# Attention on one Trainium2 core: weighted sums two key tiles behind the scores, and the transposed steps moved to the end of the turn

## The chip, the cores and the metric

The kernel runs on one core of one Trainium2 chip. The metric is the device time of one execution in microseconds (us). Before the change it is 7679.73 us, the median of three runs (7679.41 to 7688.48). The profile below is of one further execution, with a span of 7673.1 us.

The engines are named as the profile names them: PE is TensorE (matmuls), PEld its weight loads, DVE is VectorE, ACT is ScalarE, POOL is GpSimd, and SP the engine that issues DMAs.

## The reference, cut to what matters

The reference is two layers over four images of 128 channels by 64x64 pixels, that is 4096 tokens of 128 values for each image: a convolutional attention, then a multi-head attention with a feed-forward, then a recurrent layer over all tokens. The change touches only the multi-head attention:

```python
B, S, H, D = ...              # 4 images, S = 4096 tokens, 16 heads of D = 8
q      = transpose(_qz_ring(heads + rx_theta))           # queries, keys and values are the same q
scores = einsum('bhsd,bhtd->bhst', q, q) / sqrt(D)
attn   = softmax(scores, axis=-1)
ctx    = einsum('bhst,bhtd->bhsd', attn, q)
```

Queries and keys are the same vectors, so the matrix of scores of a head is symmetric. The kernel uses that: the exponentials of one off-diagonal pair of blocks are computed once, and serve the other one transposed. No maximum is subtracted ahead of the exponential.

## The kernel before, in words

**Stages.** For each of the four images, `first_stage` does the convolutional attention (with the feed-forward of the image before it in between), and `second_stage` does the multi-head attention by calling `attention` (L523). After the last image come `third_stage` and the recurrence. Inside the stages the order of TensorE, ScalarE and VectorE instructions (in the attention GpSimd's too) is exactly the order in which the Python code emits them (`manual_schedule`)[...].

**Blocks and turns.** The attention runs over 8 pairs of heads, and in each pair over 4 query blocks `b` of 1024 queries. A block meets its own 8 key tiles of 128 keys ("own" tiles), and the key tiles of the one or two blocks in `behind[b]` ("off" tiles): blocks 0 and 1 meet 16 off and 8 own tiles, in the order off, off, own; blocks 2 and 3 meet 8 and 8, in the order off, own. That is 80 tiles in a pair. One pass through the inner loop (L790), for one key tile and two heads, is called a **turn** here. In this version the instructions of a turn are emitted in this order:

1. **S**, the scores (L800): four matmuls of 32 rows, in four row tiles of the array at once, into two PSUM tiles `ss` of 128x1024, one for each head. The pool `ps_pair` has three such tiles.
2. Two exponentials on ScalarE (L809), one for each head, into `es`. Off tiles also leave a sum (`accum_out`, shown as ACTIVATION_READ_ACCUMULATOR). The `es` tiles come round again after five turns.
3. **M**, transposed ("mirror") steps (L661), through `run_pending`: the sums that the transposed exponentials give to the other block. Four off tiles make a group, and a group has 16 steps of four matmuls each, in four column tiles of the array; in float32 each is recorded as two matmuls. `credit` says how many steps a turn may run: an own turn adds 2 and an off turn 3, at most 4 are held, and what isn't used is carried over. The last step of a group is followed by a copy or an addition on VectorE that takes the sums out of PSUM (`later <- misc`, L672 or L674). The groups alternate between two halves of one tile `misc`.
4. **W**, the weighted sums (L679) of the tile of the turn before, `weigh(before)`: four matmuls (eight records) with four column tiles, into `acc`, which accumulates over the block. `ps_acc` has one tile. After a block's last tile `finish` (L703) is called; it starts with a VectorE transpose of `acc` into `o` (L707), and GpSimd then sorts the parts.
5. **Flips**, `run_flips` (L639): VectorE's 32x32-wise transposes (L648) of this turn's exponentials, if the tile is an off tile. They are what M of a later turn reads. On a block's last tile no flips are emitted.

[...]`ps_pair` holds three tiles of two banks, `ps_acc` and `ps_misc` one bank each.

Of the kernel before, what the change touches and what calls it, by code (L numbers as in the profile page):

```python
# [26 lines left out]
def kernel(  # L27
# [31 lines left out]
    nc = tc.nc  # L59
# [50 lines left out]
    def get(kind, name):  # L110
        if callable(here[kind]):
            return here[kind](name)
        pool, shape = here[kind]
        return pool.tile(shape, F32, tag=kind, name=name)
# [7 lines left out]
    def half_tile(name):  # L122
        return get("half", name)
# [399 lines left out]
    def attention(n, q, xs, tail, upcoming):  # L523
# [10 lines left out]
        fixed, _ = here["fixed"]  # L534
# [88 lines left out]
        def run_pending(turn, count):  # L623


            taken = 0
            if pending and pending[0][0] <= turn:
                steps = pending[0][1]
                while steps and taken < count:
                    steps.pop(0)()  # L630
                    taken += 1
                if not steps:
                    pending.pop(0)
            return taken
# [4 lines left out]
        def run_flips(most):  # L639
            while most and flips:  # L640
                g, k, es = flips[0]
                if g >= 2 and groups[g - 2]["steps"]:
                    return
                group = groups[g]
                if k == 0:
                    group["e"] = [get("flipped", f"t{group['name']}_{h}") for h in range(2)]
                for h in range(2):
                    nc.vector.transpose(group["e"][h][:, k, :], es[h])  # L648
                if k == TG - 1:
                    pending.append((turn + 1, group["steps"], group["block"]))  # L650
                flips.pop(0)
                most -= 1
# [21 lines left out]
                    nc.vector.tensor_tensor(dst, dst, state["acc"], ALU.add)  # L674

        def weigh(it):
            for h in range(2):
                for x in range(2):
                    nc.tensor.matmul(  # L679
                        it["acc"][ts(2 * h + x, 32), :],  # L680
                        it["qa"][:, ds((2 * it["jt"] + h) * V, 32)],
                        it["e"][h][:, ts(x, IC)],
                        start=it["first"],
                        stop=it["last"],
                        skip_group_check=True,
                    )

        def mirrored_sums(pair, b, denom):

            total = denom[:, 0, ts(b, QT), :]  # L690
            for slot in range(1, len(met_by[b])):
                by_key = small.tile([P, QT, 2], F32, tag="by_key", name=f"by_key{n}_{pair}_{b}")
                nc.gpsimd.tensor_tensor(by_key, total, denom[:, slot, ts(b, QT), :], ALU.add)
                total = by_key
            by_token = small.tile([P, QT, 2], F32, tag="by_token", name=f"by_token{n}_{pair}_{b}")
            src = total.rearrange("p (x s) h -> p s x h", s=4)
            dst = by_token.rearrange("p (x a) h -> p a x h", a=4)
            for a in range(4):
                for s in range(4):
                    nc.gpsimd.tensor_copy(dst[ts(s, 32), a], src[ts(a, 32), s])  # L700
            return by_token

        def finish(pair, b, acc, later, denom):  # L703


            o = half_tile(f"o{n}_{pair}_{b}")
            nc.vector.transpose(o, acc)  # L707

            tag = "own" if b else "own_0"
            own = once.tile([P, QT, 2, V], F32, tag=tag, name=f"own{n}_{pair}_{b}")  # L710
            ov = o.rearrange("p (s a m) -> p s a m", s=4, a=4)
            for h in range(2):
                for x in range(2):
                    for s in range(4):
                        nc.gpsimd.tensor_copy(  # L715
                            own[ts(s, 32), ts(x, 4), h, :], ov[ts(2 * h + x, 32), s, :, 0:V]
                        )

            def mirrored():
                while any(g["steps"] and g["block"] <= (pair, met_by[b][-1]) for g in groups):  # L720
                    run_flips(TG)
                    run_pending(turn + 2, 16)
                sums = mirrored_sums(pair, b, denom)


                turned = get("turned", f"turned{n}_{pair}_{b}")
                nc.vector.transpose(turned, later[:, ts(b, 2 * P)])  # L727
                tv = turned.rearrange("p (y k a d) -> p k y a d", y=2, k=4, a=4)
                other = once.tile([P, QT * 2 * D], F32, tag="other", name=f"other{n}_{pair}_{b}")
                to = other.rearrange("p (y a h d) -> p h y a d", y=2, a=4, h=2)  # L730
                for x in range(2):
                    for h in range(2):
                        for k in range(4):
                            nc.gpsimd.tensor_copy(to[ts(k, 32), h], tv[ts(2 * h + x, 32), k])  # L734
                    at = other.rearrange("p (t h d) -> p t h d", h=2, d=D)
                    nc.gpsimd.tensor_tensor(own[:, :, :, 0:D], own[:, :, :, 0:D], at, ALU.add)
                nc.gpsimd.tensor_tensor(own[:, :, :, D], own[:, :, :, D], sums, ALU.add)

            def result():
                inv = small.tile([P, QT, 2], F32, tag="inv", name=f"inv{n}_{pair}_{b}")  # L740
                nc.vector.reciprocal(inv, own[:, :, :, D])
                nc.vector.tensor_tensor(
                    qb[:, ts(b, QT), ts(pair, 2 * D)].rearrange("p t (h d) -> p t h d", d=D),
                    own[:, :, :, 0:D],
                    inv.unsqueeze(3).broadcast_to([P, QT, 2, D]),
                    ALU.mult,
                )

            if b:
                ends.append((turn, mirrored))  # L750
                ends.append((turn + 6, result))
            else:
                first.extend([mirrored, result])

        def order(b):

            own = list(range(QT * b, QT * (b + 1)))
            rest = [jt for k in behind[b] for jt in range(QT * k, QT * (k + 1))]
            each = len(rest) // QT
            return [  # L760
                jt for k in range(QT) for jt in rest[each * k : each * (k + 1)] + own[k : k + 1]
            ]
# [5 lines left out]
                return [get("exps", f"e{name}_{h}") for h in range(2)]  # L768
            return [xs[:, ts(2 * k + h, QB)] for h in range(2)]

        before = None
        turn = 0

        credit = 0.0
# [1 line left out]
        ends, first = [], []  # L776
# [3 lines left out]
        for pair in range(NPAIR):  # L780
            keys, queries, qa, later, denom = ready
            for b in range(NQB):
                acc = get("ps_acc", f"acc{n}_{pair}_{b}")
                tiles = order(b)
                end_of_all = pair == NPAIR - 1 and b == NQB - 1

# [3 lines left out]
                for at, jt in enumerate(tiles):  # L790
# [27 lines left out]

                    if at == 1:
                        credit = 4.0  # L820
                    credit -= run_pending(turn, int(credit))
                    turn += 1
                    while ends and ends[0][0] < turn:
                        ends.pop(0)[1]()
                    if before is not None:
                        weigh(before)
                        if before["last"]:
                            finish(*before["block"])

                    if b == 0 and at == 10 and pair:  # L830
                        ends.append((turn, first.pop(0)))
# [23 lines left out]
                            groups.append(group)  # L855
                        flips.append((len(groups) - 1, jt % TG, es))

                    if jt != tiles[-1]:
                        run_flips(2)
                    for _ in range(3 if tail and turn == 2 else 1):  # L860
                        if tail and turn > 1 and next(tail, tail) is tail:
# [1 line left out]
                            rest()  # L863
                    if end_of_all and at in (QT, QT + 6) and upcoming:
                        upcoming.pop(0)()
                    before = {
                        "acc": acc,
                        "qa": qa,
                        "jt": jt,
                        "e": es,  # L870
                        "first": jt == tiles[0],
                        "last": jt == tiles[-1],
                        "block": (pair, b, acc, later, denom),
                    }
                assert not coming
                w = w_next
            if pair + 1 < NPAIR:
                ready = upcoming_pair
        weigh(before)
        finish(*before["block"])  # L880
        for f in upcoming:
            f()
        while flips or pending:
# [250 lines left out]
    def second_stage(im, tail, upcoming):  # L1134
# [33 lines left out]
        with stage(f"attn{n}", sides, others, **pools):  # L1168
            engines = {e.engine for e in (nc.tensor, nc.scalar, nc.vector, nc.gpsimd)}
            with tc.manual_schedule(engines=engines):  # L1170
                im["left"] = attention(n, im["q"], im["xs"], tail, upcoming)
# [30 lines left out]
    before = None  # L1202
    x_next = {"xs": load_x(0, ts(0, P))}
    for n in range(N):
# [12 lines left out]
        before = image  # L1217
# [22 lines left out]
    with stage("runs", t2=((P, 2 * IC), 4 * N), half=(HALF, 2 * NS + 1), ps_one=(ONE, 2 * NS)):  # L1240
# [34 lines left out]
        with tc.manual_schedule(engines={nc.tensor.engine, nc.scalar.engine}):  # L1275
# [3 lines left out]
            for t in range(-WARM, L):  # L1279
                for k in range(NS):  # L1280
                    acc = wx[k].rearrange("p (n i c) -> p n i c", n=NN, c=IC // L)
# [145 lines left out]
```

## Time and profile before

| stretch of the span, us | what | length, us | PE busy, us | ACT busy, us | DVE busy, us |
|---|---|---|---|---|---|
| 446 to 1761 | attention, image 0 | 1315 | 1299.30 | 1275.00 | 973.81 |
| 2330 to 3636 | attention, image 1 | 1306 | 1288.60 | 1262.92 | 966.19 |
| 4206 to 5509 | attention, image 2 | 1303 | 1288.00 | 1262.47 | 964.53 |
| 6076 to 7388 | attention, image 3 | 1312 | 1294.41 | 1266.07 | 970.05 |
| the rest | convolution, feed-forward, recurrence | 2437 | | | |

The four attention stretches are 5236 us of the 7673.1 us, and the change concerns only these. PE's busy time in the profile is modelled, since matmuls are pipelined; a PE that is shown busy for 99% of a stretch need not be at its peak. The better measure is how far apart the first score matmuls of two successive turns start: that is the length of a turn on TensorE. In the same way, the distance between the starts of two exponentials is what ScalarE takes for one. Wait lines read "engine, waiting line <- engine, line waited for: us in total, times, longest".

### The profile page before, as it was taken

The numbers are of one execution on the slowest core, as the hardware profiler recorded it, in microseconds if no ns is written. First come the engines' busy times: TensorE is split into PE (matmuls) and PEld (weight loads), VectorE is DVE, ScalarE is ACT, GpSimd is POOL, SyncE is SP. The second block draws the span as 40 slices with busy tenths as digits, with TensorE's granted clock in tenths as the row PEclk, the third lists the DMA queues.
The fourth block names the chain that finished last, engine by engine and source line by source line (L and its number), as shares of the span: only waits on it lengthen the run. The fifth ranks groups of instructions, "written<-read, shape, count | busy, mean of one in ns | idle before, by whom it ended". The sixth has DMA issues, their size and how long they took to land. (4 is left out here: it accounts for less than half of the span.)

```text
span 7673.1 us, 211342 instructions
## 1 busy us (share of the span) xinstructions
PE 7342.2 (96%) x87566; PEld 3334.3 (43%) x87566; DVE 5561.2 (72%) x7344; ACT 6146.6 (80%) x9493; POOL 2769.3 (36%) x9796
## 2 busy tenths in 40 slices
PE   8999999999999999999899999999999999999976
PEld 3334444444444444444444444444444444444445
DVE  5777777776787777777678777777677877777754
ACT  4479999995448999999444999999844699999964
POOL 1134444343223433343323343444322334444341
PEclk9999999999999999999999999999999999999987
DMA  0010000000111000000011000000001100000012
GB/s 26 25 42 23 25 19 20 19 9 24 33 44 36 25 20 19 23 21 16 18 33 46 32 20 19 22 23 17 17 25 34 52 20 23 23 25 19 11 53 102
DMA packets 81501, 211.92 MB, mean 28 GB/s; under 512 B 8768, under 2 KB 8800, under 8 KB 79760
## 3 DMA queue, kind: packets, MB, share of 16 engines
q1 hardware_dynamic: 77312, 186.68, 7.1%
q8 instruction: 689, 11.29, 0.6%
q10 hardware_dynamic: 2016, 10.49, 0.3%
q14 instruction: 284, 2.33, 0.1%
q0 software_dynamic: 1200, 1.14, 0.1%
HBM read 141.65 MB, written 56.62 MB: 26 GB/s over the span
## 5 line engine op out<-in xcount | busy, mean ns | idle before, releaser
L809 ACT ACTIVATE e<-s 128x1024 f32<-128x1024 f32 x3104 | 3068.5, 1027 | 117.1 <-PE s L800 104.8
L648 DVE STREAM_TRANSPOSE t<-e 128x1024 f32<-128x1024 f32 x1872 | 2201.4, 1218 | 653.4 <-ACT e L809 635.8
L809 ACT ACTIVATE xs<-s 128x1024 f32<-128x1024 f32 x2016 | 1993.0, 1025 | 49.4 <-PE s L800 46.3
L661 PE MATMUL misc<-t,mirror 128*32 128x128 f32 x49152 | 1817.9, 278 | 55.4 <-DVE later L672 27.6
L679 PE MATMUL acc<-e,q_aug 128*32 128x512 f32 x12416 | 1700.9, 595 | 0.0
L648 DVE STREAM_TRANSPOSE t<-xs 128x1024 f32<-128x1024 f32 x1200 | 1413.2, 1218 | 357.8 <-ACT xs L809 346.0
L661 PEld LDWEIGHTS misc<-t,mirror 128*32 128x32 f32 x49152 | 1225.5, 110 | 609.1 <-issue 450.9
L800 PEld LDWEIGHTS s<-queries,keys 32*128 32x128 f32 x10240 | 502.7, 181 | 2154.4 <-issue 1712.8
L715 POOL COPY own<-o 32x36 f32<-32x36 f32 x2048 | 428.6, 209 | 2768.7 <-DVE o L707 2688.8
L800 PE MATMUL s<-queries,keys 32*128 32x512 f32 x10240 | 1312.5, 495 | 11.0 <-ACT e L809 8.8
L679 PE MATMUL acc<-xs,q_aug 128*32 128x512 f32 x8064 | 1148.2, 595 | 0.0
L388 PE MATMUL acc<-p,asmT 128*128 128x512 f32 x2048 | 975.1, 610 | 0.0
L373 ACT ACTIVATE p<-s 128x1024 f32<-128x1024 f32 x512 | 497.0, 1022 | 519.9 <-PE s L365 512.7
L381 DVE TENSOR_TENSOR total<-total,p 128x1024 f32<-128x1024 f32 x448 | 578.0, 1290 | 243.8 <-ACT p L373 220.4
L618 POOL COPY mirror<-q 32x128 f32<-32x128 f32 x2048 | 595.2, 291 | 94.7 <-PE misc L661 6.8
L388 PEld LDWEIGHTS acc<-p,asmT 128*128 128x128 f32 x2048 | 364.2, 191 | 543.8 <-issue 541.5
L365 PE MATMUL s<-e,e 64*128 64x512 f32 x2048 | 531.6, 639 | 4.6 <-ACT p L373 3.0
L734 POOL COPY other<-turned 32x64 f32<-32x64 f32 x2048 | 472.2, 231 | 95.7 <-DVE turned L727 9.9
L679 PEld LDWEIGHTS acc<-e,q_aug 128*32 128x32 f32 x12416 | 390.1, 110 | 91.3 <-issue 42.8
L809 ACT ACTIVATION_READ_ACCUMULATOR e<-s 128x1 f32 x1872 | 388.7, 208 | 0.0
L679 PEld LDWEIGHTS acc<-xs,q_aug 128*32 128x32 f32 x8064 | 259.0, 109 | 112.0 <-issue 55.0
L365 PEld LDWEIGHTS s<-e,e 64*128 64x128 f32 x2048 | 181.9, 192 | 278.2 <-issue 251.1
(237 smaller groups left out, 4901.8 us busy)
## 6 DMA issues: line engine op xcount, KB each, us to landing
keys<-parts_dram SPq DMA_DIRECT2D x256, 256.0 KB
queries<-parts_dram SPq DMA_DIRECT2D x1024, 32.0 KB
fx<-x_dram SPq DMA_DIRECT2D x64, 256.0 KB
x_dram<-x SPq DMA_DIRECT2D x56, 256.0 KB
xs<-in_x_dram SPq DMA_DIRECT2D x16, 512.0 KB
t_dram<-t2T SPq DMA_DIRECT2D x32, 256.0 KB
t2s<-t_dram SPq DMA_DIRECT2D x16, 512.0 KB
parts_dram<-high SPq DMA_DIRECT2D x28, 256.0 KB
```

The costliest lines, as they stand in the source:

```text
L365: nc.tensor.matmul(s[:, j, :], e2[rows, ts(2 * jp + j, P)], e1[rows, ts(ic, IC)], start=True, stop=True,)
L373: nc.scalar.activation(p, s, AF.Exp)
L381: nc.vector.tensor_tensor(state[ic], state[ic], p, ALU.add)
L388: nc.tensor.matmul(state["acc", ic], asmT[:, ts(2 * jp + j, P)], p[:, j, :], start=jp == 0 and j == 0, stop=jp == NP - 1 and j == 1,)
L618: nc.gpsimd.tensor_copy(wv[ts(a, 32), s, :, :, ts(a, D)], own[ts(s, 32)])
L648: nc.vector.transpose(group["e"][h][:, k, :], es[h])
L661: nc.tensor.matmul(state["acc"][ts(2 * h + x, 32), :], state["w"][:, QT * (s // 4) + TG * x + s % 4, h, :], state["e"][h][:, :, ds(IC * x ...
L679: nc.tensor.matmul(it["acc"][ts(2 * h + x, 32), :], it["qa"][:, ds((2 * it["jt"] + h) * V, 32)], it["e"][h][:, ts(x, IC)], start=it["first ...
L715: nc.gpsimd.tensor_copy(own[ts(s, 32), ts(x, 4), h, :], ov[ts(2 * h + x, 32), s, :, 0:V])
L734: nc.gpsimd.tensor_copy(to[ts(k, 32), h], tv[ts(2 * h + x, 32), k])
L800: nc.tensor.matmul(ss[h][:, x, :], keys[jt // QT].bitcast(F32R)[r, cols], queries[b].bitcast(F32R)[r, :], start=True, stop=True,)
L809: nc.scalar.activation(es[h], ss[h].rearrange("p x c -> p (x c)"), AF.Exp, scale=1.0 / math.sqrt(D), accum_out=denom[:, slot, jt, h : h + ...
```

## The change

Two things move. First, W runs two tiles behind S instead of one: `before`, a single remembered tile, becomes the list `waiting` of two. Second, W is emitted directly behind S, ahead of M, so that TensorE's order in turn k becomes S(k), W(k-2), M in place of S(k), M, W(k-1). The idea is that W should find its exponentials long finished, so that TensorE doesn't stop on it ahead of the next scores.

What follows from it in the code: the tile `acc` of a block is now taken only when the block's first W is emitted (the block's last W of before comes at the next block's second turn), `finish` is called one turn later, at the next block's second turn, and the turn in which no flips are emitted moves from a block's last turn to its first. The amount of work on every engine is unchanged.

```diff
         def weigh(it):
+            if it["first"]:
+                it["in"]["acc"] = get("ps_acc", "acc{}_{}_{}".format(n, *it["block"]))
             for h in range(2):
                 for x in range(2):
                     nc.tensor.matmul(
-                        it["acc"][ts(2 * h + x, 32), :],
+                        it["in"]["acc"][ts(2 * h + x, 32), :],
...
-        def finish(pair, b, acc, later, denom):
+        def finish(pair, b, block, later, denom):
             o = half_tile(f"o{n}_{pair}_{b}")
-            nc.vector.transpose(o, acc)
+            nc.vector.transpose(o, block["acc"])
...
-        before = None
+        waiting = []
...
-                acc = get("ps_acc", f"acc{n}_{pair}_{b}")
+                block = {"acc": None}
...
                     if at == 1:
                         credit = 4.0
+
+                    if len(waiting) == 2:
+                        it = waiting.pop(0)
+                        weigh(it)
+                        if it["last"]:
+                            finish(*it["block"])
                     credit -= run_pending(turn, int(credit))
                     turn += 1
                     while ends and ends[0][0] < turn:
                         ends.pop(0)[1]()
-                    if before is not None:
-                        weigh(before)
-                        if before["last"]:
-                            finish(*before["block"])
...
-                    if jt != tiles[-1]:
+                    if at:
                         run_flips(2)
...
-                    before = {
-                        "acc": acc,
+                    fresh = {
+                        "in": block,
...
+                    waiting.append(fresh)
...
-        weigh(before)
-        finish(*before["block"])
+        for it in waiting:
+            weigh(it)
+        finish(*it["block"])
```

More of the change, by code (lines that the diff above doesn't have):

```diff
@@ L872, in attention @@
                         "last": jt == tiles[-1],
-                        "block": (pair, b, acc, later, denom),
+                        "block": (pair, b, block, later, denom),
                     }
+                    waiting.append(fresh)
                 assert not coming
```

## The prediction

> **What bounds the kernel now.** I read the page first: shares, slices, costliest groups.
>
> ```profile
> PE 7342.2 (96%) x87566; PEld 3334.3 (43%) x87566; DVE 5561.2 (72%) x7344; ACT 6146.6 (80%) x9493; POOL 2769.3 (36%) x9796
> ...
> PE   8999999999999999999899999999999999999976
> ...
> ACT  4479999995448999999444999999844699999964
> ...
> L809 ACT ACTIVATE e<-s 128x1024 f32<-128x1024 f32 x3104 | 3068.5, 1027 | 117.1 <-PE s L800 104.8
> L648 DVE STREAM_TRANSPOSE t<-e 128x1024 f32<-128x1024 f32 x1872 | 2201.4, 1218 | 653.4 <-ACT e L809 635.8
> ```
>
> In the attention slices both PE and ACT stand at 9: two engines at their limit, so the busy shares don't name one bound. ACT's idle time ahead of the exponentials ends mostly with scores, and DVE waits for exponentials: the circle is S, exponential, W/M. The chain of waits is of no use (it stops in the recurrence's end). So I took starts from the trace, turn by turn.
>
> PE: from one S to the next, a turn with n mirror steps takes 1.43 us (n=0, the shortest of 392), 1.66, 1.87, 2.09, 2.30 (n=4, the shortest of 504): **1.43 + 0.217n**. With the counts seen (392, 192, 508, 948, 504) that makes 4955 us; those turns took 5232. So PE stops for 277 us, 157 of it in turns without M (mean 1.83) and 97 in turns with four (mean 2.49).
>
> ACT: exponentials start 1.013 us apart in off turns and 0.92 in own turns (medians): 3072 x 1.013 + 2048 x 0.92 = 4996 us, against 5275 spent. **Each engine loses some 280 us to the other.** How they lose it is in the order of time:
>
> ```profile
> 2881.14 0.51 PE L800 MATMUL s<-queries,keys 32*128 32x512 f32 x4
> ...
> 2881.58 1.29 PE L679 MATMUL acc<-xs,q_aug 128*32 128x512 f32 x8
> ...
> 2882.80 0.19 PEld L800 LDWEIGHTS s<-queries,keys 32*128 32x128 f32 x4 [0.84 <-issue]
> ```
>
> ```profile
> 2892.20 3.45 DVE L648 STREAM_TRANSPOSE t<-xs 128x1024 f32<-128x1024 f32 x3
> ...
> 2895.18 0.50 PE L800 MATMUL s<-queries,keys 32*128 32x512 f32 x4
> 2895.58 0.25 DVE L674 TENSOR_TENSOR later<-later,misc 128x128 f32<-128x128 f32 x1
> 2895.88 0.81 PEld L661 LDWEIGHTS misc<-t,mirror 128*32 128x32 f32 x32 [0.51 <-DVE later L674]
> ...
> 2897.75 0.19 PEld L800 LDWEIGHTS s<-queries,keys 32*128 32x128 f32 x4 [0.84 <-issue]
> ...
> 2898.35 1.02 ACT L809 ACTIVATE e<-s 128x1024 f32<-128x1024 f32 x1 [0.35 <-PE s L800]
> ```
>
> First: a turn without M. W follows S at once, and its eight matmuls take 1.29 us instead of the 1.04 of other turns: the second head's exponential isn't there yet, and the next S stands behind it. Second: a turn of four steps. M stops 0.27 us (its weights load 0.70 us after S, elsewhere 0.43) on VectorE's L674, itself behind three flips; W and the next S come late, and ACT waits 0.35 us.
>
> **What the Trainium skill says.** "TensorE: Matmul & The Clock Gate", Part 2: weight loads may be pulled ahead, but "The MATMULs themselves stay in program order". The first fence agrees: S behind a waiting W is late, 1.66 us a turn and not 1.43. "TensorEngine Tiling (Array Packing)", Tiling Modes: "Changing tiling mode (not just tile) drains the TensorE". It shows: the two passes of W start 0.43 us apart, but S comes 0.54 after the second. M and W share a mode (128 rows x 32 columns). "PSUM — Partial Sum Buffer", PSUM bank collisions: guard PSUM by bank and quadrant, not by address. So M must wait for the copy of the other half of `misc`, as it does above. The same page, Engine vs sequencer instructions: VectorE's queue is strictly first in, first out; hence L674 behind the flips (it starts at 2895.58, where they end).
>
> **The change, part by part.**
>
> *Instruction counts* are the same on every engine: 0.
>
> *S, W, M in place of S, M, W.* A turn still has two mode switches, S to 128x32 and back. W directly behind S exists in the trace: turns of 1.43 us, on the same line. W to M and M to S don't occur. Low end 0; high end one more drain of 0.54 - 0.43 = 0.11 us a turn. I take 0: the drain behind M replaces that behind W, and W to M is no mode switch.
>
> *W two tiles back* never waits: S(k) already needed the PSUM tile that the first exponential of turn k-1 frees, so those of k-2 are done. That removes the 0.24 us of the turns without M wherever PE is late. It also lets PE work ahead. Before, with W(k-1) held until the second exponential of k-1, S follows 0.98 us later (2881.58 + 0.24 to 2882.80) and is usable 0.55 after that; ACT wants it 2.03 (off) or 1.84 us after the same point: a lead of 0.3 to 0.5 us. After, PE is held only at S(k)'s second head, for the end of the first exponential of k-1; the next S is due 1.43 us later and wanted 1.01 + 2.03 - 0.55 = 2.49 later: **a lead of 1.0 us**.
>
> *M last* starts 1.0 us later in its turn (S 0.43 and W 0.86 ahead instead of S alone; W ran behind it anyway). The wait of 0.27 us for flips and copy then falls away in the middle of blocks.
>
> *`finish` and `acc`.* The transpose `o` starts 1.22 us after the last W's start. That W is now 0.44 us behind S(1) of the next block, so `o` starts at 1.66 us; now it starts 0.14 after S(1). Queued behind it on VectorE: flips of tiles 0 and 1, then 3 and 4, which M of turn 6 wants. The next W into `acc` is at S(2) + 0.44 = 2.30 + 0.44 = 2.74 us; `o` ends at 1.66 + 0.72 = 2.38: hidden. The flips: 1.66 + 0.64 + 8 x 1.13 + 0.2 (a copy) = 11.5 us in block 1, 11.9 in block 0 (transpose L727 besides, 0.33). M of turn 6 is ready at 2.30 + 1.87 + 2.08 + 2.08 + 1.43 + 0.43 + 0.86 = 11.05, and its first 0.1 us needs only the first head: **a stall of 0.35 and 0.7 us**, where it was 0.28. Blocks 2 and 3 have four off tiles in eight turns: none.
>
> *Sum by block*, measured medians against what is left:
> - Block 1: 24 turns, 64 steps, PE floor 24 x 1.43 + 64 x 0.217 = 48.2; ACT 32 x 1.013 + 16 x 0.92 = 47.1. PE-bound. Measured 49.69. After: 48.2 + 0.35, less the 0.2 lead of block 0's end: 48.4, rounded up to 48.5.
> - Block 0: same floor, measured 49.45. The stall of 0.7 is mostly paid from the lead that it starts with: 48.3.
> - Block 2: ACT floor 30.9, PE 16 x 1.43 + 32 x 0.217 = 29.8. Measured 32.29. It starts without lead; its first five turns (4, 4, 3, 2, 3 steps) take PE 10.63 and ACT 9.77: 0.86 lost. Three turns without M then bring the lead to 1.0, and the rest costs nothing: 31.8.
> - Block 3: measured 32.01, starts with a lead of 1.0, which covers the 0.86: 31.1.
>
> 163.44 becomes 159.7 us: 3.74 a pair, x 32 pairs = 120 us. 7680 - 120 = **7560 us**. The ends of the images wait for flips and final M as now: 0.
>
> **Rivals.**
> - *Everything hides*: 48.2 twice and 30.9 twice, 158.2 a pair, 5.24 x 32 = 168: 7512. For it: both engines have the time. Against: `o` is later on a VectorE that runs nearly without gaps ahead of turn 6.
> - *VectorE takes it back*: `o` and the flips stall the long blocks by 1 us more than I have, and hold a first W. Gains of 0.3, 0.3, 0.2, 0.6: 1.4 x 32 = 45: 7635. For it: flips start 1.13 us apart there, and M's wait sits on them now. Against: idle time of 653 us before flips over the run.
> - *Switching costs more*: 0.11 us in each turn of the PE-bound long blocks, 1536 x 0.11 = 169 lost, 120 gained: 7729, slower. For it: never measured in this trace. Against: the count of switches doesn't change.
>
> **How the numbers follow.** Forecast 0.55, everything hides 0.15, VectorE 0.18, slower 0.12. The range takes in the first three with some room: 7500 to 7650. Slower by over 0.2%: 0.11; within 0.2%, the edges of the last two: 0.04; faster: 0.85.
>
> **What would show it.** Turns on the same line 1.43 + 0.217n prove the switches free; a line 0.1 higher proves the last rival. Turns without M in long blocks at 1.43 to 1.55, not 1.66. M's wait for L672/L674 (139 us in all) nearly gone, its wait for flips (25 us) grown, at turn 6. ACT's waits for S, 151 us, about halved. I'd be wrong if the clock granted to PE in the attention (1.00) fell, or if W waited for `o`.

## The result, and the profile after

The changed kernel takes 7636.23 us, the median of four runs (7633.59 to 7642.2); the kernel before, on the same chip, 7683.31 us (7679.41 to 7688.48). The ratio is 0.9939, with a 95% interval of 0.9922 to 0.9957: **47 us faster, 0.6%**, where 120 us were forecast. A second measurement, as the control of the experiments, gave 0.9938.

The page of the changed kernel, the same lines as shown of before (in this kernel S is L802, the exponentials L811, W L681, `o` L709):

```profile
PE 7337.4 (96%) x87566; PEld 3449.0 (45%) x87566; DVE 5523.6 (72%) x7344; ACT 6146.8 (81%) x9493; POOL 2766.9 (36%) x9796
...
L811 ACT ACTIVATE e<-s 128x1024 f32<-128x1024 f32 x3104 | 3068.9, 1027 | 93.5 <-PE s L802 78.0
L648 DVE STREAM_TRANSPOSE t<-e 128x1024 f32<-128x1024 f32 x1872 | 2187.7, 1214 | 447.4 <-ACT e L811 435.8
```

PE's and ACT's busy times are those of before, as they must be. What moved is the waits; here from the list of waits, first of the kernel before, then of the changed one (engine, waiting line, what it waited for: us in total, times, longest):

```profile
PEld s L800 <- issue: 1712.8, 2048, 1.7
PEld s L800 <- PE misc L661: 415.8, 496, 0.8
...
DVE o L707 <- PE acc L679: 260.5, 125, 2.1
...
ACT e L809 <- PE s L800: 104.8, 224, 8.3
...
DVE inv L741 <- POOL own L737: 41.1, 25, 10.8
```

```profile
DVE o L709 <- PE acc L681: 420.8, 125, 3.5
...
PEld s L802 <- ACT e L811: 229.2, 516, 2.3
PEld s L802 <- ACT xs L811: 225.6, 355, 1.6
...
DVE inv L743 <- POOL own L739: 174.1, 96, 10.8
...
ACT e L811 <- PE s L802: 78.0, 161, 6.5
```

TensorE's weight loads for S now have 455 us put down to exponentials, where it was 28 us. That is not the time for which TensorE is held: some 324 us of it are gaps of 0.84 us ahead of an S that follows a W directly. Before the change such a gap stood ahead of nearly every S, and the list put it down to "issue" or to M. What is left, 196 gaps of 0.30 us in the middle of an S among it, shows that TensorE does run ahead at times and is then held. ScalarE's waits for scores fell from 151 us to 89. And two waits grew on VectorE: for the last W of a block ahead of `o` (260 to 421 us), and for GpSimd ahead of the reciprocal of `result` (41 to 174 us).

For where the time went, turns are a better measure than waits. Since TensorE now runs ahead at times, I take the turns of ScalarE (from the first exponential of a turn to the first of the next; medians below) and measure a block from its first exponential to the next block's first exponential (mean over the six middle head pairs of every image; the forecast column is the prediction's own):

| block | before, us | forecast, us | after, us | missed by, us |
|---|---|---|---|---|
| 0 (24 turns) | 49.48 | 48.3 | 49.18 | 0.9 |
| 1 (24 turns) | 49.69 | 48.5 | 48.84 | 0.3 |
| 2 (16 turns) | 32.26 | 31.8 | 31.92 | 0.1 |
| 3 (16 turns) | 32.02 | 31.1 | 31.94 | 0.8 |
| a pair | 163.45 | 159.7 | 161.88 | 2.2 |

(163.45 - 161.88) x 32 pairs = 50 us, close to the measured 47. The largest gain is in block 1; blocks 0 and 2 gained 0.3 us each, and block 3 hardly anything. Outside the attention, where the code is the same, the profiled execution took 2413 us where it took 2398 before; the other runs have 2397 to 2418 there, so this tells nothing of the change.

**Block 1: the part that worked.** The two stops of before are gone in its later turns: turns 12, 18 and the next block's 0 take ScalarE 2.19 to 2.22 us instead of 2.47. The turn without M takes TensorE 1.43 us instead of 1.67.

**Turn 6 of the long blocks: VectorE.** The trace of the changed kernel in block 1, first the start of `o`, then turn 6:

```profile
2861.20 0.50 PE L802 MATMUL s<-queries,keys 32*128 32x512 f32 x4
...
2861.64 1.07 PE L681 MATMUL acc<-xs,q_aug 128*32 128x512 f32 x8
...
2862.77 0.72 DVE L709 STREAM_TRANSPOSE o<-acc 128x512 f32<-128x512 f32 x1 [3.24 <-PE acc L681]
```

```profile
2870.34 2.35 DVE L648 STREAM_TRANSPOSE t<-xs 128x1024 f32<-128x1024 f32 x2
...
2871.60 1.07 PE L681 MATMUL acc<-xs,q_aug 128*32 128x512 f32 x8
...
2872.48 1.33 PE L661 MATMUL misc<-t,mirror 128*32 128x128 f32 x32
...
2873.74 0.19 PEld L802 LDWEIGHTS s<-queries,keys 32*128 32x128 f32 x4 [0.20 <-issue]
...
2874.35 1.03 ACT L811 ACTIVATE e<-s 128x1024 f32<-128x1024 f32 x1 [0.31 <-PE s L802]
```

`o` starts 1.57 us behind S, and VectorE had nothing to do for 3.24 us ahead of it. Then the flips run without a gap until 2872.69, while M's first weights load at 2872.05; its 32 matmuls take 1.33 us instead of the 1.06 of an unheld four-step turn, and ScalarE waits 0.31 us.

**Block 3's first turn: the lead.** TensorE enters it ahead of ScalarE, with scores ready before they are wanted:

```profile
2938.50 2.85 ACT L811 ACTIVATE xs<-s 128x1024 f32<-128x1024 f32 x3
2939.08 0.18 PEld L802 LDWEIGHTS s<-queries,keys 32*128 32x128 f32 x2 [0.84 <-ACT e L811]
...
2939.58 0.25 PEld L802 LDWEIGHTS s<-queries,keys 32*128 32x128 f32 x2 [0.31 <-ACT xs L811]
2940.07 0.16 PEld L681 LDWEIGHTS acc<-e,q_aug 128*32 128x32 f32 x8 [0.24 <-issue]
...
2941.94 0.19 PEld L802 LDWEIGHTS s<-queries,keys 32*128 32x128 f32 x4 [0.20 <-issue]
```

S is torn in two: the first head's weights load at 2939.08, those of the second 0.50 us later, when the end of an exponential releases them, as the prediction had it for the third PSUM tile. (Over the middle pairs the halves lie 0.50 us apart here, 0.49 in block 0's first turn and in turns 7 and 8 of blocks 2 and 3, and 0.01 in most other turns.) W and four steps of M stand behind the second half, and so the next S comes at 2941.94, 2.36 us after it. A turn of four steps without any such hold takes 2.31 us. On ScalarE block 3's first two turns took 2.18 and 2.36 us before the change, and 2.17 and 2.36 after it: the lead bought nothing.

### The profile page after: what moved, and what is told of

Read it like the earlier page. It is cut to its first block, busy times and chain, and to the rows that moved or that the text cites. A ratio compares the mean times of both kernels' runs of the same rounds, so it can differ in the third digit from the quotient of the medians.

```text
span 7634.5 us, 211357 instructions
## 1 busy us (share of the span) xinstructions
PE 7337.4 (96%) x87566; PEld 3449.0 (45%) x87566; DVE 5523.6 (72%) x7344; ACT 6146.8 (81%) x9493; POOL 2766.9 (36%) x9796
## 5 line engine op out<-in xcount | busy, mean ns | idle before, releaser
L811 ACT ACTIVATE e<-s 128x1024 f32<-128x1024 f32 x3104 | 3068.9, 1027 | 93.5 <-PE s L802 78.0
L661 PEld LDWEIGHTS misc<-t,mirror 128*32 128x32 f32 x49152 | 1448.7, 110 | 1331.4 <-issue 1232.7
L811 ACT ACTIVATE xs<-s 128x1024 f32<-128x1024 f32 x2016 | 1993.1, 1025 | 21.8 <-PE s L802 10.6
L661 PE MATMUL misc<-t,mirror 128*32 128x128 f32 x49152 | 1771.4, 274 | 22.6 <-POOL mirror L553 8.4
L681 PE MATMUL acc<-e,q_aug 128*32 128x512 f32 x12416 | 1663.1, 607 | 0.0
L802 PE MATMUL s<-queries,keys 32*128 32x512 f32 x10240 | 1450.3, 496 | 8.4 <-ACT e L811 6.5
L681 PE MATMUL acc<-xs,q_aug 128*32 128x512 f32 x8064 | 1074.6, 605 | 0.0
L802 PEld LDWEIGHTS s<-queries,keys 32*128 32x128 f32 x10240 | 567.7, 182 | 848.3 <-issue 384.4
L681 PEld LDWEIGHTS acc<-e,q_aug 128*32 128x32 f32 x12416 | 247.4, 108 | 386.9 <-issue 374.5
L709 DVE STREAM_TRANSPOSE o<-acc 128x512 f32<-128x512 f32 x128 | 91.6, 716 | 420.8 <-PE acc L681 420.8
L811 ACT ACTIVATION_READ_ACCUMULATOR e<-s 128x1 f32 x1872 | 388.7, 208 | 0.0
```

The costliest lines, as they stand in the source:

```text
L661: nc.tensor.matmul(state["acc"][ts(2 * h + x, 32), :], state["w"][:, QT * (s // 4) + TG * x + s % 4, h, :], state["e"][h][:, :, ds(IC * x ...
L681: nc.tensor.matmul(it["in"]["acc"][ts(2 * h + x, 32), :], it["qa"][:, ds((2 * it["jt"] + h) * V, 32)], it["e"][h][:, ts(x, IC)], start=it[ ...
L802: nc.tensor.matmul(ss[h][:, x, :], keys[jt // QT].bitcast(F32R)[r, cols], queries[b].bitcast(F32R)[r, :], start=True, stop=True,)
L811: nc.scalar.activation(es[h], ss[h].rearrange("p x c -> p (x c)"), AF.Exp, scale=1.0 / math.sqrt(D), accum_out=denom[:, slot, jt, h : h + ...
```

## The experiments

Two theories were on the table. **Theory 1**: the lead can't be carried into turns with many M steps, and besides VectorE stalls the long blocks. **Theory 2**: VectorE alone took the gain back, as the prediction's second rival said (it named 7635 us, which is what was measured).

| kernel | block 0 | 1 | 2 | 3 | pair, us | time, us | ratio to before (95%) |
|---|---|---|---|---|---|---|---|
| changed, as control | 49.18 | 48.84 | 31.92 | 31.94 | 161.88 | 7636.9 | 0.9938 (0.9925 to 0.9952) |
| flips at once | 49.00 | 48.56 | 31.92 | 31.94 | 161.41 | 7622.27 | 0.9921 (0.9907 to 0.9934) |
| steps spread | 49.18 | 48.83 | 30.51 | 30.71 | 159.24 | 7552.48 | 0.983 (0.9817 to 0.9844) |
| both | 49.15 | 48.56 | 30.94 | 31.13 | 159.78 | 7570.2 | 0.9852 (0.9837 to 0.9867) |
| two behind only | 51.59 | 51.37 | 32.22 | 31.99 | 167.17 | 7793.8 | 1.0144 (1.0127 to 1.0161) |
| order only | 51.83 | 51.77 | 33.91 | 34.16 | 171.68 | 7944.79 | 1.0336 (1.0319 to 1.0353) |
| before, steps spread | 49.53 | 49.69 | 30.84 | 30.79 | 160.85 | 7601.1 | 0.989 (0.9873 to 0.9906) |
| spread, flips in long blocks | 49.06 | 48.57 | 30.51 | 30.71 | 158.85 | 7544.03 | 0.9816 (0.9802 to 0.9829) |
| and result later | 48.59 | 48.56 | 30.51 | 30.71 | 158.37 | 7531.89 | 0.98 (0.9786 to 0.9813) |
| and three at most | 48.64 | 48.46 | 30.54 | 30.73 | 158.38 | 7526.47 | 0.9791 (0.9777 to 0.9804) |

**The control.**

> The changed kernel again, beside the three others on the same chip: 7636 us, ratio to before 0.994, under every theory.

**Flips at once.**

```diff
-                    if at:
-                        run_flips(2)
+                    run_flips(2)
```

> The changed kernel, but flips are emitted in every turn, the first turn of a block too, so that tile 0's flips stand ahead of the transpose o on VectorE instead of behind it. Theory 1 (two causes: the lead of TensorE can't be used because S splits over the third PSUM tile, and VectorE's chain stalls M in turn 6 of the long blocks): only the second cause goes. The idle VectorE time ahead of o takes in two flips, M of turn 6 no longer waits, ScalarE gets back about 0.55 us in block 0 and 0.25 us in block 1, 0.8 x 32 = 26 us: about 7610 us. Blocks 2 and 3 unchanged at 31.9 us. Theory 2 (VectorE alone takes the gain back, as the second rival of the prediction has it): the whole missing 75 us come back, about 7560 us. Theory 3 (o behind the flips holds the first W): no gain, or slower than the changed kernel.

Measured 7622 us: 15 us of the 26 expected, and far from the 60 further ones of theory 2. Turn 6 is cured in both long blocks (ScalarE's turn falls from 2.76 to 2.15 us in block 0, from 2.42 to 2.15 in block 1), block 1 gains the 0.28 us. But in block 0 turn 12 now takes 2.61 us instead of 2.19, so that most of its share is lost again; what waits there is found below. VectorE's stall at turn 6 is real, but curing it alone doesn't bring the forecast back.

**Steps spread.** In blocks 2 and 3 a turn runs at most two steps:

```diff
-                    credit = min(credit + (3.0 if off else 2.0), 4.0)
+                    most = 4.0 if b < NQB // 2 else 2.0
+                    credit = min(credit + (3.0 if off else 2.0), most)
                     if at == 1:
-                        credit = 4.0
+                        credit = most
```

> The changed kernel, but in blocks 2 and 3 a turn runs at most two mirror steps (credit held at 2 there), so that their 32 steps lie evenly in 16 turns instead of 4, 4, 3, 2, 3, 0, 0, 0. Theory 1: bunching costs what the lead was to cover, 0.9 us in each of blocks 2 and 3; with 1.87 us a turn TensorE is always below ScalarE's mean of 1.93, both blocks fall to ScalarE's 31.0 us, 1.8 x 32 = 58 us: about 7578 us. Theory 2 (VectorE alone) and the prediction's own account (a lead of 1.0 us covers block 3): block 3 gains nothing by it, the whole at most 0 to 25 us: 7611 to 7636 us.

Measured 7552 us, 84 us under the control. Block 3, which by the prediction's account had nothing to gain, gains 1.23 us, block 2 1.41. Theory 2 falls. That is more than theory 1 had, since ScalarE's floor was set too high: where it never has to wait for scores, its turns take 1.99 (off) and 1.81 us (own), 30.4 us for 16, and not 30.9. The kernel before had shown it: turns 6 and 7 of its blocks 2 and 3 take just that. Of the 392 turns without M, in which TensorE mostly waits, 48 are left; turns of two steps, 1.87 us, which is less than ScalarE's mean turn, take their place.

**The same on the kernel before.**

> The kernel before, with only the spreading: at most two mirror steps a turn in blocks 2 and 3. Theory 1: the evenness, not the lead, is what these blocks want; they fall from 32.3 and 32.0 us to about 31.1, 2.1 x 32 = 67 us: about 7615 us, more than the change brought. Rival (W two tiles behind is needed for the blocks to reach ScalarE's floor, since W one tile behind waits): at most 30 us, 7650 us or more.

Measured 7601 us: the spreading alone brings 81 us, more than the change, with W one tile behind as ever. Blocks 2 and 3 fall to 30.84 and 30.79. So the lead isn't needed to bring these blocks within 0.4 us of ScalarE's floor of 30.4; evenness is. On top of the spreading the change still brings some 49 us (7601 to 7552): in a pair 0.86 us in block 1, 0.35 in block 0 and 0.33 in block 2.

**Both edits.**

> Both edits: flips in every turn, and the mirror steps of blocks 2 and 3 spread two to a turn. Theory 1: the causes are separate, so the gains add, 26 + 58 = 84 us: about 7552 us, pair sum near 159.2 us. Theory 2: no more than flips at once give alone.

Measured 7570 us, 18 us more than spreading alone: the gains don't add. The third theory of "flips at once" (`o` behind the flips holds the first W) is right after all, for the short blocks. Turn 2 of block 3 in this kernel's trace:

```profile
2918.49 2.37 DVE L648 STREAM_TRANSPOSE t<-xs 128x1024 f32<-128x1024 f32 x2 [1.29 <-ACT xs L811]
...
2920.39 0.55 PE L802 MATMUL s<-queries,keys 32*128 32x512 f32 x4
2920.79 0.68 DVE L709 STREAM_TRANSPOSE o<-acc 128x512 f32<-128x512 f32 x1
...
2921.52 0.64 PE L681 MATMUL acc<-xs,q_aug 128*32 128x512 f32 x4 [0.58 <-DVE o L709]
```

With two steps a turn, S of turn 2 comes 1.87 us after that of turn 1, and no longer 2.30; `o`, behind two flips, ends too late, and the block's first W waits 0.58 us for `acc`. The Trainium skill's "PSUM — Partial Sum Buffer", Engine vs sequencer instructions, has VectorE's queue as strictly first in, first out; here it shows as an `o` whose input is ready and which waits for the two flips ahead of it.

**Two tiles behind only** (W back behind M, still two tiles late):

```diff
+                    credit -= run_pending(turn, int(credit))
+                    turn += 1
+                    while ends and ends[0][0] < turn:
+                        ends.pop(0)[1]()
                     if len(waiting) == 2:
                         it = waiting.pop(0)
                         weigh(it)
                         if it["last"]:
                             finish(*it["block"])
-                    credit -= run_pending(turn, int(credit))
-                    turn += 1
-                    while ends and ends[0][0] < turn:
-                        ends.pop(0)[1]()
```

> Half of the change: W two tiles behind, but in its old place after M (S, M, W). Theory 1: W never waits, but o comes 2.5 us behind S of turn 1 (S 0.43, M 0.87, W 1.22) and the flips behind it end 12.4 us after it, while M of turn 6 is ready 10.4 us after it: a stall of 2.0 us in each long block, and the 0.27 us waits of M for its copy stay. About 2.6 us a pair slower, x 32 = 83: about 7765 us. Rival (going two tiles behind is what brings the gain, the place of M nothing): 7640 us or less.

Measured 7794 us, 1.4% slower than before. One thing more differs in this kernel: `finish` stands behind the loop over `ends` again, but is called in a block's second turn, so that `mirrored` and `result`, the end of a block's work, are emitted a turn later than in the kernel before and in the changed one. The loss is where it was expected: turn 6 takes 4.45 us in block 0 and 4.13 in block 1, instead of 2.50 and 2.48; M's matmuls wait 178 us for flips, weight loads and matmuls together, where it was 25. The short blocks don't change.

**Order only** (W directly behind S, but of the turn before):

```diff
-                    if len(waiting) == 2:
+                    if len(waiting) == 1:
...
-                    if at:
+                    if jt != tiles[-1]:
                         run_flips(2)
```

> The other half: W directly behind S and M last, but W still one tile behind (S, W of the turn before, M). Theory 1: W now stands 0.44 us behind S, and the second exponential of the turn before ends later than that, so TensorE can't have a turn under about 2.2 us (off) or 2.0 us (own): 2.3 us more in a long block and 1.5 in a short one, 7.6 x 32 = 243: about 7925 us (7850 to 8000). Rival (the place of M is what brings the gain): 7640 us or less.

Measured 7945 us, 3.4% slower than before. A part of the mechanism is in TensorE's own waits, from this kernel's list:

```profile
PEld acc L681 <- ACT e L811: 103.4, 339, 0.8
PEld acc L681 <- ACT xs L811: 81.7, 256, 0.4
```

W waits for exponentials 185 us, where it was 86 before, and turns 8 and 10 of the long blocks take 2.11 and 2.20 us, where they took 1.87 and 2.03. That is close to the expected limits of 2.0 us for an own and 2.2 us for an off turn. Turn 8 of blocks 2 and 3 was not expected: 3.02 and 3.24 us, where both took 2.20 before. The trace of such a turn in block 2:

```profile
2868.37 0.26 DVE L743 RECIPROCAL inv<-own 128x16 f32<-128x16 f32 x1 [1.97 <-POOL own L739]
...
2868.95 2.36 DVE L648 STREAM_TRANSPOSE t<-xs 128x1024 f32<-128x1024 f32 x2
...
2871.36 0.80 PEld L661 LDWEIGHTS misc<-t,mirror 128*32 128x32 f32 x28 [0.69 <-DVE t L648]
...
2872.90 1.94 ACT L811 ACTIVATE e<-s 128x1024 f32<-128x1024 f32 x2 [0.85 <-PE s L802]
```

VectorE's reciprocal stands 1.97 us for GpSimd, the flips behind it are late, M waits for them, and ScalarE then waits 0.85 us. This belongs to a side effect of the edit: `finish` is called ahead of `turn += 1` in a block's first turn, so `result`, which holds the reciprocal, is emitted one turn earlier than in the kernel before and in the changed one. By the two turns' excess (0.8 and 1.0 us a pair) it makes some 59 of the 263 us; that is an estimate, as no run has the order without it.

Each half alone, as built here, makes the kernel slower; only both together are a gain. My reading is that M last pays for `o` coming later (the stall of turn 6 shrinks from 2 us to a few tenths), and W two tiles behind pays for W standing directly behind S.

**Spread, flips at once in the long blocks only.** `if at or b < NQB // 2:` in place of `if at:`.

> The changed kernel with the steps of blocks 2 and 3 spread, and flips in the first turn of blocks 0 and 1 only, so that o stays ahead of the flips in the short blocks. Theory (o behind the flips held the first W of blocks 2 and 3 in the run with both edits, 0.43 us each; in the long blocks the flips fit ahead of o): the short blocks go back to 30.5 and 30.7 us, block 1 stays at 48.56, block 0 at 49.0 since a second VectorE wait, in turn 12, remains; pair sum 158.8 us, 7538 us. Rival (the two edits disturb each other in another way): no better than spreading alone, 7552 us.

Measured 7544 us: the short blocks are back at 30.51 and 30.71, blocks 0 and 1 at 49.06 and 48.57, as expected. Block 0 keeps its wait in turn 12, and in this kernel's trace its origin is seen, over seven microseconds ahead of it:

```profile
2800.09 0.24 POOL L739 TENSOR_TENSOR own<-own,by_token 128x16 f32<-128x16 f32 x1
...
2800.36 0.25 DVE L743 RECIPROCAL inv<-own 128x16 f32<-128x16 f32 x1 [1.97 <-POOL own L739]
...
2800.93 1.23 DVE L648 STREAM_TRANSPOSE t<-e 128x1024 f32<-128x1024 f32 x1
...
2807.72 0.25 DVE L672 COPY later<-misc 128x128 f32<-128x128 f32 x1
...
2808.02 0.81 PEld L661 LDWEIGHTS misc<-t,mirror 128*32 128x32 f32 x32 [1.18 <-DVE later L672]
```

VectorE stands idle for 1.97 us on GpSimd, whose sorting begins with `o` and therefore later than before: in block 0 `o` starts 3.6 us behind the block's first exponential, where it was 1.8. The flips behind it are late, run on without a gap, and the copy of `misc` behind them holds M.

**And `result` later.**

```diff
-                ends.append((turn + 6, result))
+                ends.append((turn + 8, result))
```

> As before it, and the two VectorE instructions of result (reciprocal and product) two turns later, at turn + 8. Theory: in block 0 the reciprocal stands at the head of VectorE's queue waiting for GpSimd's sums, which start later since o does, and the flips behind it make M of turn 12 wait (0.6 us for 0.16): with result later that wait goes, block 0 falls to 48.5 to 48.6, 0.4 x 32 = 13 us, 7525 us. Rival (turn 12 waits for something else, the transpose of later at turn 11 or the copy of the sums): no change from the run beside it.

Measured 7532 us: the reciprocal's wait for GpSimd falls from 199 to 38 us, turn 12 from 2.68 to 2.20 us, block 0 from 49.06 to 48.59. The cause is shown by its removal. Together with the flips at once this takes 0.60 us out of block 0 and 0.27 out of block 1, 28 us by the pairs, 20 by the times (7552 to 7532).

**And three steps at most in the long blocks.**

> As before it, and at most three mirror steps in a turn in blocks 0 and 1 too, so that 16 steps come as 3, 3, 2, 3, 3, 2 and not 4, 3, 2, 3, 3, 1. Theory: these blocks are bound by TensorE's sum (48.2 us), which doesn't change; only what ScalarE adds on top of it, 0.3 us a block, can go: 0 to 20 us, 7505 to 7525 us. Rival (unevenness costs as much here as in blocks 2 and 3): 30 us or more.

Measured 7526 us, an interval that overlaps with the run beside it, and the same pair sum: nothing to be had that stands clear of the noise. These blocks are bound by TensorE's sum (48.2 us against 48.5 to 48.6 measured), not by its distribution. The last two kernels are the best, about 2% under the kernel before and 1.4% under the changed one.

## Why the prediction was wrong, point by point

- **The bound** (two engines in lock, each losing 280 us to the other): right in kind; the best kernels get 154 and 160 us of it back. But ScalarE's floor was mis-sized. The 1.013 and 0.92 us are medians over all turns, also those around which ScalarE waited for scores; in turns 6 and 7 of blocks 2 and 3 of the same trace, where it was not kept waiting, two exponentials take 1.99 and 1.81 us. A block of 16 turns has 30.4 us as its floor, and not 30.9. That block 2 came out within 0.1 us of its forecast is luck: "the rest costs nothing" is wrong as well (its turns 8 to 13 lose 0.6 us against 1.99 and 1.81), and the two errors cancel.
- **The new order costs nothing in itself**: right. Turns of TensorE lie on the same line as before, 1.43, 1.65, 1.87, 2.09 and 2.31 us (medians for 1 to 4 steps, shortest for 0). The rival with dearer switching is out. "TensorEngine Tiling (Array Packing)", Tiling Modes, of the Trainium skill has TensorE drained by a change of mode, not by one of tile alone; W and M share a mode (128x32), and the step from W to M shows no cost here.
- **W never waits, M's wait for its copy goes**: right, and that is the gain in block 1. W's waits for exponentials fall from 86 to 4 us. M's for its copy fall from 139 to 65 us, and what is left are mostly gaps of 0.30 us, which other loads of M show too; the turns of four steps no longer lose by it (2.31 us).
- **A lead of 1.0 us: the step that failed.** I took it from the moment at which TensorE is held to the next S of a turn *without* M, 1.43 us later, against 2.49 us when ScalarE wants it. Then I charged a four-step turn only the 0.27 us by which it is longer than ScalarE's. But the 0.87 us of its own four steps come out of the same 1.0 us: S, W, M and the next S all start from the held second half of S. By the figures, 1.43 + 0.87 = 2.30 of 2.49 us; in the trace 2.36, and the next exponential came 0.1 us late. A lead of 0.8 to 1.0 us was to cover two four-step turns and to pass into block 0; it was used up before the first of them was over. That missed 0.8 us in block 3. In block 0 it left the stall of turn 6, which the lead was to pay for, to ScalarE: 0.6 us, which is what the cure of turn 6 took out of that turn. 1.4 x 32 = 45 of the missing 73 us; the rest is spread over blocks 0 to 2 and isn't assigned further. The spreading shows that bunched steps are what these blocks lose by; that the PSUM tile is what holds TensorE is read from the trace, and no run has more or fewer of these tiles.
- **VectorE's stall at turn 6**: right in place, and nearly in size: its cure gives ScalarE 0.6 and 0.27 us back in turn 6, against the 0.7 and 0.35 forecast. But in block 0 I had it paid from the lead; turn 6 took 2.76 us there, 0.26 more than before. The sign I had named, a longer wait of M for flips in the list, didn't show (25 us before, 23 after); the length of turn 6 shows the stall.
- **`finish` a turn later hides**: right for `acc` (no W of the changed kernel waits for `o`); but I looked only at VectorE behind `o`, and not at GpSimd behind it. The later sums hold the reciprocal (174 us for 41), in the changed kernel behind the stall at turn 6, and in the open once that is cured.
- **The second rival** named the measured time, but not the cause: curing VectorE's turn 6 brings 15 us, curing the reciprocal too some 20 to 28, spreading the steps 84. By blocks it was off: it gave block 1 a gain of 0.3 us and block 3 one of 0.6, and they gained 0.85 and 0.08. That its sum fits is luck.
- **The clock**, named as a sign of being wrong: 0.99 to 1.00 in the attention stretches, where it was 1.00. The trace has 41 us at half speed in them, all near the start of an image, and had 27 before. If half of the difference was lost, that is 7 us of the missing 73.

## What to carry to other kernels

When two engines pass tiles back and forth through a few PSUM buffers, work that is merely reordered need not give the slack that it seems to: count the lead from the point at which the leading engine is held, with all the work that stands between that point and the next hand-over. Even out the work per turn first; here that was worth more than the deeper pipeline, and needed three lines. And when an operation moves later, follow everything that hangs on it on every engine, as both the flips and GpSimd's sums did on `o`.

## What I had not expected

The time shown for one exponential rises when ScalarE is better fed: in the kernel with spread steps the mean is 1092 ns instead of 1027, and along a block 2 it climbs from 1.03 to over 1.2 us. Yet the exponentials start 0.996 and 0.904 us apart all along, as in the few turns of the kernel before in which ScalarE didn't wait, and ScalarE's busy time as a whole falls (6146.6 to 6089.7 us). So its floor is better read from the distance of starts in stretches where it is never starved. And the idle time of PEld with the mark "issue" moved from S (1713 to 384 us) to M (451 to 1233 us) without any effect on the length of a turn: the loads of S show a gap of 0.84 us behind W and of 0.20 behind M, so such gaps follow the order of the work, and are no loss by themselves.
